# One product for two groups, the third group's scan first, and dt*u in halves

## The chip, the cores and the metric

The kernel runs on one core of one Trainium2 chip. The metric is the device time of one execution in microseconds (us). Engine names are those of the profile: PE is the matmul engine, DVE the vector engine, ACT the scalar engine, POOL is GpSimd, and SP issues nearly all DMAs.

## The reference, cut to what matters

The network has four layers on four images of 56 x 56 pixels and 96 channels. Layers 0 and 1 hold a selective scan; layers 2 and 3 hold linear attention and a quantized feed-forward part. Nearly all the time goes to the scans, and the change is in them. For each image the 3136 tokens are scanned in four directions, with 192 inner channels and 16 states a channel:

```python
d_a = jnp.exp(dt[..., None] * a)                 # decay, one per channel, state, token
d_b = dt[..., None] * b_ssm[:, :, None, :]
def step(h, inp):
    da_t, db_t, x_t, c_t = inp
    h = da_t * h + db_t * x_t[..., None]         # h = decay*h + (dt*u)*B
    y_t = jnp.einsum('bds,bs->bd', h, c_t)       # y = sum over states of h*C
```

The outputs of the four directions are added and go on to the gates, projections and normalizations of the layer.

## The kernel before, in words

**Chunks and rounds.** A direction's 3136 tokens are cut into 7 chunks of 448 tokens. Two layers, four images, four directions and seven chunks make 224 chunks. Each chunk has eight *rounds* r = 0..7: the two halves e of the inner channels (96 each) times the four quarters q of the states. A round handles 32 channels x 4 states on the 128 partitions, for NG = 3 *groups* of channels. So there are 1792 rounds, and two of the four directions read the image by columns (`orient` 1), where `U` is read with a stride.

**One round n, in `scans`.** `products(n)` multiplies du (that is dt*u, spread over the partitions) by B for the groups 0 and 1 on DVE; B lies in the PSUM bank `b`, where PE put it (`spread_b`, line 606). Group 2's product is made on POOL, one round ahead, in `begin(n + 1)` (line 699), with B and C from the tile `cb` in SBUF. `scan(n, g)` (line 711) runs the recurrence on DVE for g = 0, 1, 2, in place in the tile `h`, with the decays from the PSUM bank `da[g]`; after each scan ACT makes the next round's decay of that group in the same bank (`decay`, line 663). After the third scan ACT keeps the last column (`kept`, line 681) and later puts it in front of the next chunk's tile (`carried`, line 676). POOL then multiplies h by C for all three groups at once (line 753, tile `hc`), and two rounds later PE adds the states up (`add_up`, line 784) behind a filling of matmuls on zeros (`keep_busy`, line 771).

**The order is written out by hand.** DVE, PE, ACT and POOL take their instructions in the order of the program, each in one queue. In a round POOL's queue holds: line 753 of the round before, then whatever `prepare` put there, then line 699 for the next round, then line 753 of this round. Line 753 waits for the round's last scan.

**What is prepared ahead.** For every chunk `prepare(ch, o)`, `prepare_on_scalar(ch, o)` and `on_tensor(ch, o)` are called with o from -14 up: o = -1 is the last round before the chunk's first. At o = -7 and -6 ACT makes dt = softplus in the tile `dtc` (two Exp and, at -6, one Ln over both halves, line 498). At o = -5 `times_u` makes `duc` = dt*u on POOL, both halves in one instruction of 96 x 896 elements (line 511), and `park` sends `dtc` to DRAM in three DMAs of SP. At o = -4 `duc` is parked likewise. `spread_dt` and `spread_du` fetch both back onto 128 partitions, for e = 0 at -4 and -3, for e = 1 at 0. `fetch` brings `cb` at -3 to 0. In terms of the chunk in front, o = -6, -5, -4, -3 are its rounds 2, 3, 4, 5.

**Work beside the rounds.** The rest of the network runs as *lanes*: generators that are moved on at the `yield` of each half round, as far as a planner's budget for ACT and PE allows. Their instructions stand between the scans of DVE, and in the queues of the others.

Of the kernel before, what the change touches and what calls it, by code (L numbers as in the profile page):

```python
# [11 lines left out]
F32 = mybir.dt.float32  # L12
# [4 lines left out]
ALU = mybir.AluOpType  # L17
# [3 lines left out]
HS = 56  # L21
L = HS * HS
C = 96
DI = 192
NS = 16
NE = 2
NG = 3
NQ = 4
# [4 lines left out]
CS = 448  # L33
# [134 lines left out]
class Net:  # L168
# [333 lines left out]
        t = self.sp.tile([rows, 2 + n * CS], F32, name=name, bufs=bufs)  # L502
        return t[:, 2:].rearrange("p (n t) -> p n t", t=CS)

    def times_u(self, ch):

        ch.duc = self.sp.tile([C, NE, CS], F32, name="duc", bufs=1)
        u = self.both.rearrange("p e (h w) -> p e w h" if ch.orient else "p e (h w) -> p e h w", w=HS)
        lo = ch.c * CS // HS
        in_rows = lambda t: t.rearrange("p e (a b) -> p e a b", b=HS)  # L510
        self.nc.gpsimd.tensor_tensor(in_rows(ch.duc), in_rows(ch.dtc), u[:, :, lo : lo + CS // HS], ALU.mult)  # L511

    def park(self, t):
        d = self.dram.tile([NE, 32, NG, CS], F32, tag="dd", name="dd", bufs=6)
        for g in range(NG):
            self.nc.sync.dma_start(d[:, :, g].rearrange("e d t -> d e t"), t[32 * g : 32 * g + 32])
        return d

    def spread(self, t, d):
# [25 lines left out]
    def prepare(self, ch, o):  # L545

        nc = self.nc
        if o == -14:  # L550
            self.parameters(ch)
        elif o == -12:
            self.inputs(ch)
        elif o == -9:
            ch.cd = self.dram.tile([2 * NS, CS], F32, tag="cd", name="cd", bufs=3)
            nc.sync.dma_start(ch.cd, ch.cf[: 2 * NS])
        elif o == -5:
            self.times_u(ch)
            ch.dtd = self.park(ch.dtc)
        elif o == -4:  # L560
            ch.dud = self.park(ch.duc)
            self.spread_dt(ch, 0)
        elif o == -3:
            self.spread_du(ch, 0)
        elif o == 0:
            self.spread_du(ch, 1)
            self.spread_dt(ch, 1)
        if -3 <= o <= 0:
            self.fetch(ch, o + 3)
# [43 lines left out]
    def scans(self):  # L613

        nc, sp = self.nc, self.sp
        chunks = []
        for l in range(2):
            for i in range(NB):
                for n, (orient, rev) in enumerate(ORDER[l]):
                    for step in range(NCS):
                        ch = Step()
                        ch.l, ch.i, ch.orient, ch.rev, ch.step = l, i, orient, rev, step
                        ch.k = 2 * orient + rev if l == 0 else orient + 2 * rev
                        ch.c = NCS - 1 - step if rev else step  # L630
                        ch.n, ch.first = n, n == 0 and step == 0
                        ch.skip = n == 0
                        ch.last = n == 3 and step == NCS - 1
                        ch.cb, ch.dt, ch.du = [], [], []
                        chunks.append(ch)
        rounds = [(ch, e, q) for ch in chunks for e in range(NE) for q in range(NQ)]
        per = NE * NQ


        da = [self.psum.tile([128, 512], F32, name=f"da{g}")[:, : CS + 4] for g in range(NG)]  # L640
        for t in da:
            nc.vector.memset(t, 0.0)

        def steps(n):

            return [(ch, n - per * j) for j, ch in enumerate(chunks[max(0, n // per) : n // per + 3], max(0, n // per))]

        def ahead(n):
            for ch, o in steps(n):
                self.on_tensor(ch, o)  # L650

        for n in range(-14, 0):
            for ch, o in steps(n):
                self.prepare(ch, o)
            for ch, o in steps(n):
                self.prepare_on_scalar(ch, o)
            ahead(n)

        def decay(n, g):

            if n < len(rounds):
                ch, e, q = rounds[n]
                nc.scalar.activation(da[g][:, INNER], ch.dt[e][:, g], AF.Exp, scale=ch.par.na[:, e, q, g : g + 1])  # L663

        def column(t, at):

            return t[:, at : at + 2 * ROW + 1 : ROW]

        def carried(n):

            if n < len(rounds):
                ch, e, q = rounds[n]
                hs[n] = sp.tile([128, WIDE], F32, name="h", bufs=3)
                if not ch.step:
                    return
                nc.scalar.copy(column(hs[n], ROW if ch.rev else 1), ch.par.carry[:, e, q])  # L676

        def kept(n):
            ch, e, q = rounds[n]
            if ch.step < NCS - 1:  # L680
                nc.scalar.copy(ch.par.carry[:, e, q], column(hs[n], 2 if ch.rev else CS + 1))  # L681

        def own(n):
            ch, e, q = rounds[n]
            return NQ * e + q in (OWN_TAIL if ch.l and ch.i else OWN)

        hs, bs = {}, {}

        def tokens(t):

            return self.groups(t, 2)[:, :, :CS]

        def begin(n):

            if n < len(rounds):
                ch, e, q = rounds[n]
                bs[n] = self.spread_b(ch, q)
                if not own(n):
                    nc.gpsimd.tensor_tensor(tokens(hs[n])[:, 2], ch.du[e][:, 2], ch.cb[q][:, 1], ALU.mult)  # L699

        def products(n):
            ch, e, q = rounds[n]
            for g in range(3 if own(n) else 2):
                nc.vector.tensor_tensor(tokens(hs[n])[:, g], ch.du[e][:, g], bs[n], ALU.mult)  # L704

        def scan(n, g):
            ch, e, q = rounds[n]
            c = 1 if ch.step else 0
            way = slice(CS + 1 + c, 1, -1) if ch.rev else slice(2 - c, CS + 2)
            h = hs[n][:, g * ROW :]  # L710
            nc.vector.tensor_tensor_scan(h[:, way], da[g][:, way], h[:, way], 0.0, ALU.mult, ALU.add)  # L711

        carried(0)
        carried(1)
        begin(0)
        self.exp_and_ln()
        self.tables = True
        for g in range(NG):
            decay(0, g)
        late = []  # L720
        for n, (ch, e, q) in enumerate(rounds):
            r = NQ * e + q
            products(n)
            for c, o in steps(n):
                self.prepare(c, o)
            self.half_round()
            strided = [1.5 + 1.5 * ch.orient] * (r % NQ == 2)
            strided += [1.5 + 1.5 * c.orient for c, o in steps(n) for _ in self.projected(c, o)]
            self.spend((0.6, 0.7, 1.7, 0, 0, 0, 0.7, 0.6)[r], (1.3, 1.3, 0, 0, 0, 0, 0.4, 0.4)[r] + sum(strided))
            yield "F", n, r  # L730
            for c, o in steps(n):
                self.prepare_on_scalar(c, o)
            ended = late.pop(0) if len(late) == 2 else None
            if ended:
                self.keep_busy(ended[2])
            begin(n + 1)
            if ended:
                self.add_up(*ended)
            ahead(n)
            self.half_round()  # L740
            for g in range(NG):
                if g == 1:
                    yield "C", n, r
                if g == 2 and ended and ended[2] == NQ - 1:
                    self.spend(0.6, 0)
                    self.keep_sums(*ended[:3])
                scan(n, g)
                if g == 2:
                    kept(n)
                decay(n + 1, g)  # L750
            carried(n + 2)
            hc = sp.tile([128, NG, CS], F32, name="hc", bufs=3)
            nc.gpsimd.tensor_tensor(  # L753
                hc, tokens(hs[n]), ch.cb[q][:, 0].unsqueeze(1).to_broadcast([128, NG, CS]), ALU.mult,
            )
            late.append((ch, e, q, hc))
            del hs[n], bs[n]
        for ended in late:
            self.add_up(*ended)
        self.keep_sums(ch, e, q)  # L760
        yield "C", len(rounds), 0
# [647 lines left out]
```

## Time and profile before

| | |
|---|---|
| median of 3 runs | 8133.2 us (8116.01 to 8143.82) |
| the profiled execution | 8146.18 us, of which the span from first to last instruction is 8144.5 us |
| busy, share of the span | DVE 92%, PE 88%, POOL 88%, ACT 75% |
| scan phase (116 to 7934 us) | 7818 us; DVE busy 7445 us, POOL 7138 us |
| granted PE clock | 0.901 |
| SP's DMA issues of `dtc` and `duc` to DRAM | 672 each, 112 KB, 2.0 us to landing |

A group's line on the page names the line of the kernel, the engine, the operation, what is written and read, the shapes and the count; after the first bar stand the busy time in us and the mean of one instruction in ns; after the second the idle time of the engine just before it and what ended it. Consecutive DVE instructions overlap in the record, so the distance from start to start is shorter than the duration of one.

### The profile page before, as it was taken

Reading aid. Unit: us, or ns where it says so; the run is one execution under the profiler, and the core shown is the slowest. Engines: PE = TensorE matmul, PEld = TensorE weight load, DVE = VectorE, ACT = ScalarE, POOL = GpSimd, SP = SyncE. Lnnn points to the kernel's source line nnn. Section 1 sums busy time; section 2 is a strip of 40 time slices with the busy share of each in tenths; the row PEclk is TensorE's granted clock in tenths of the full one; section 3 lists DMA queues with packets and bytes.
Section 4 is the critical chain, followed back from the end, with each engine's and each line's share of the span. In section 5 each row is a group of like instructions: output and inputs, shape, how many; then the busy total and the mean of one; then the engine's idle time right before and its main releaser. Section 6 shows DMA issues by size and latency. Waiting matters only on the chain.

```text
span 8144.5 us, 112387 instructions
## 1 busy us (share of the span) xinstructions
PE 7161.1 (88%) x33234; PEld 2500.2 (31%) x33234; DVE 7523.2 (92%) x9600; ACT 6106.9 (75%) x12765; POOL 7170.7 (88%) x3991
## 2 busy tenths in 40 slices
PE   6889988889888988889889889988899988999887
PEld 3333333222332223322332223333233322433233
DVE  5999999999999999999999998999989999899992
ACT  5878877777778767887777866687767877678776
POOL 4999998999999999999989998899978999888980
PEclk8999989889999989999888998888989899888987
DMA  4555655567556655566555665555655556545552
GB/s 152 177 192 192 198 187 182 177 190 231 186 183 192 208 193 179 179 198 197 193 183 178 195 220 173 164 164 169 193 174 168 170 167 195 175 160 165 172 168 66
DMA packets 568237, 1467.47 MB, mean 180 GB/s; under 512 B 108035, under 2 KB 337157, under 8 KB 566757
## 3 DMA queue, kind: packets, MB, share of 16 engines
q1 hardware_dynamic: 566848, 1458.49, 56.0%
q8 instruction: 261, 4.28, 0.2%
q14 instruction: 356, 2.91, 0.1%
q10 hardware_dynamic: 772, 1.80, 0.1%
HBM read 1186.49 MB, written 273.47 MB: 179 GB/s over the span
## 4 chain that ended last, share of the span: by engine, by line
PE 33%; DVE 30%; ACT 17%; issue 13%; POOL 4%; DMA 2%; SPq 0%; DVEq 0%; POOLq 0%; ACTq 0%
DVE h L711 22%; PE y L784 7%; DVE h L704 7%; PE y L771 5%; ACT da L663 5%; PE y L780 4%; PE b L606 3%; POOL hc L753 2%; PE pp L486 2%; ACT L815 2%; PE ps L932 1%; PE pp L440 1%; PE ps L860 1%; PE ps L845 1%; ACT Y L791 1%
## 5 line engine op out<-in xcount | busy, mean ns | idle before, releaser
L711 DVE TENSOR_TENSOR_SCAN h<-da,h 128x449 f32<-128x449 f32 (+1 forms) x5376 | 5517.9, 1076 | 98.5 <-ACT da L663 81.7
L753 POOL TENSOR_TENSOR hc<-h,cb 128x1344 f32<-128x1344 f32 x1792 | 4884.6, 2726 | 617.1 <-DVE h L711 489.7
L663 ACT ACTIVATE da<-dt,na 128x448 f32<-128x448 f32 x5376 | 3354.0, 632 | 1126.1 <-DVE h L711 1095.6
L704 DVE TENSOR_TENSOR h<-du,b 128x448 f32<-128x448 f32 x3584 | 2026.8, 609 | 150.2 <-PE b L606 87.8
L784 PE MATMUL y<-hc,four 128*32 128x448 f32 x14336 | 1917.6, 610 | 17.8 <-POOL hc L753 17.8
L699 POOL TENSOR_TENSOR h<-du,cb 128x448 f32<-128x448 f32 x1792 | 1755.1, 979 | 71.9 <-ACT h L676 26.4
L771 PE MATMUL y<-w,zeros 128*96 128x448 bf16 x5112 | 1420.5, 396 | 0.0
L606 PE MATMUL b<-cf,sel 128*128 128x448 bf16 x1792 | 676.8, 378 | 698.1 <-DVE h L704 691.3
L771 PEld LDWEIGHTS <-zeros 128*96 128x96 bf16 x5112 | 631.1, 134 | 1174.8 <-issue 1014.7
L440 PE MATMUL pp<-U,wd 96*128 96x448 f32 x896 | 667.2, 833 | 11.4 <-issue 4.4
L784 PEld LDWEIGHTS y<-hc,four 128*32 128x32 f32 x14336 | 294.7, 113 | 1198.2 <-issue 687.3
L780 PE MATMUL y<-Y,ident 96*96 96x448 f32 x672 | 540.5, 894 | 36.9 <-ACT Y L791 18.7
L486 PE MATMUL pp<-cf,wd 12*96 12x448 f32 (+1 forms) x896 | 480.8, 618 | 89.7 <-ACT dtc L496 54.0
L681 ACT COPY carry<-h 128x3 f32<-128x3 f32 x1536 | 302.1, 197 | 262.6 <-DVE h L711 256.7
L511 POOL TENSOR_TENSOR duc<-dtc,U 96x896 f32<-96x896 f32 x224 | 483.0, 2156 | 11.1 <-ACT dtc L498 11.1
L791 ACT COPY Y<-y 96x448 f32<-96x448 f32 x448 | 342.0, 763 | 24.2 <-PE y L784 23.0
L676 ACT COPY h<-carry 128x3 f32<-128x3 f32 x1536 | 280.0, 182 | 52.2 <-POOL hc L753 49.3
L496 ACT ACTIVATE dtc<-pp,wd 96x448 f32<-96x448 f32 x448 | 281.5, 628 | 19.3 <-PE pp L486 15.1
L577 ACT COPY cf<-pp 64x448 f32<-64x448 f32 x448 | 235.6, 526 | 79.8 <-PE pp L599 71.5
L606 PEld LDWEIGHTS <-sel 128*128 128x128 bf16 x1792 | 184.3, 103 | 350.8 <-issue 282.2
L845 PEld LDWEIGHTS ps<-avg,w 96*112 96x112 f32 (+2 forms) x1936 | 250.4, 194 | 93.2 <-issue 55.3
L486 PEld LDWEIGHTS pp<-cf,wd 12*96 12x96 f32 (+1 forms) x896 | 114.3, 166 | 471.1 <-ACT dtc L496 163.9
(384 smaller groups left out, 5698.4 us busy)
## 6 DMA issues: line engine op xcount, KB each, us to landing
cb<-cd SPq DMA_DIRECT2D x896, 448.0 KB, 4.5
dt<-dd SPq DMA_DIRECT2D x448, 672.0 KB, 5.7
du<-dd SPq DMA_DIRECT2D x448, 672.0 KB, 5.5
dd<-dtc SPq DMA_DIRECT2D x672, 112.0 KB, 2.0
dd<-duc SPq DMA_DIRECT2D x672, 112.0 KB, 2.0
win<-m SPq DMA_DIRECT2D x252, 112.0 KB, 4.2
U<-u SPq DMA_DIRECT2D x112, 168.0 KB, 4.8
w<-z SPq DMA_DIRECT2D x84, 224.0 KB, 4.0
```

Source lines behind the costliest of these rows:

```text
L440: self.nc.tensor.matmul(ch.ps.rearrange("p (a b) -> p a b", b=HS), ch.par.wx[:, e], self.in_order(self.U[e], ch.orient, ch.c * CS, CS), st ...
L486: self.nc.tensor.matmul(ch.pd, ch.par.wt[rows, C * e : C * e + C], ch.cf[rows], start=True, stop=True)
L511: self.nc.gpsimd.tensor_tensor(in_rows(ch.duc), in_rows(ch.dtc), u[:, :, lo : lo + CS // HS], ALU.mult)
L606: self.nc.tensor.matmul(ps, self.sel[:, q], self.upper(ch.cf), start=True, stop=True)
L663: nc.scalar.activation(da[g][:, INNER], ch.dt[e][:, g], AF.Exp, scale=ch.par.na[:, e, q, g : g + 1])
L699: nc.gpsimd.tensor_tensor(tokens(hs[n])[:, 2], ch.du[e][:, 2], ch.cb[q][:, 1], ALU.mult)
L704: nc.vector.tensor_tensor(tokens(hs[n])[:, g], ch.du[e][:, g], bs[n], ALU.mult)
L711: nc.vector.tensor_tensor_scan(h[:, way], da[g][:, way], h[:, way], 0.0, ALU.mult, ALU.add)
L753: nc.gpsimd.tensor_tensor(hc, tokens(hs[n]), ch.cb[q][:, 0].unsqueeze(1).to_broadcast([128, NG, CS]), ALU.mult,)
L771: self.nc.tensor.matmul(self.y[:C], self.zeros[:, :C], self.some, start=False, stop=False)
L780: nc.tensor.matmul(o, w, self.in_order(a, ch.orient, ch.c * CS, CS), start=True, stop=False)
L784: nc.tensor.matmul(self.y[32 * n : 32 * n + 32], self.four, hc[:, g], start=n == 3, stop=n == 3 or q == NQ - 1,)
```

## The change

In each round DVE makes the product of the groups 0 and 1 in one instruction of 128 x 2 x 448, with B repeated by a step of zero. The scans run in the order 2, 0, 1 in place of 0, 1, 2; all that hangs on a place in this loop (`kept`, `keep_sums`, the lanes' turn) keeps its place. `times_u` is split into one instruction of 96 x 448 for each half, at o = -6 and -5, and stands in POOL's queue behind line 699 of that round instead of in front of it. `park` is split into halves too, both still in the same step: six DMAs of 56 KB in place of three of 112 KB, for `dtc` and for `duc`.

```diff
-    def times_u(self, ch):
-        ch.duc = self.sp.tile([C, NE, CS], F32, name="duc", bufs=1)
...
-        self.nc.gpsimd.tensor_tensor(in_rows(ch.duc), in_rows(ch.dtc), u[:, :, lo : lo + CS // HS], ALU.mult)
+    def times_u(self, ch, e):
+        if e == 0:
+            ch.duc = self.sp.tile([C, NE, CS], F32, name="duc", bufs=1)
+        in_rows = lambda t: t[:, e].rearrange("p (a b) -> p a b", b=HS)
+        u = self.in_order(self.U[e], ch.orient, ch.c * CS, CS)
+        self.nc.gpsimd.tensor_tensor(in_rows(ch.duc), in_rows(ch.dtc), u, ALU.mult)
 
-    def park(self, t):
-        d = self.dram.tile([NE, 32, NG, CS], F32, tag="dd", name="dd", bufs=6)
+    def park(self, t, e, d=None):
+        if e == 0:
+            d = self.dram.tile([NE, 32, NG, CS], F32, tag="dd", name="dd", bufs=6)
         for g in range(NG):
-            self.nc.sync.dma_start(d[:, :, g].rearrange("e d t -> d e t"), t[32 * g : 32 * g + 32])
+            self.nc.sync.dma_start(d[e, :, g], t[32 * g : 32 * g + 32, e])
...
         elif o == -5:
-            self.times_u(ch)
-            ch.dtd = self.park(ch.dtc)
+            ch.dtd = self.park(ch.dtc, 0)
+            self.park(ch.dtc, 1, ch.dtd)
         elif o == -4:
-            ch.dud = self.park(ch.duc)
+            ch.dud = self.park(ch.duc, 0)
+            self.park(ch.duc, 1, ch.dud)
             self.spread_dt(ch, 0)
...
+        def u_products(n):
+            for ch, o in steps(n):
+                if o in (-6, -5):
+                    self.times_u(ch, o + 6)
...
         def products(n):
             ch, e, q = rounds[n]
-            for g in range(3 if own(n) else 2):
-                nc.vector.tensor_tensor(tokens(hs[n])[:, g], ch.du[e][:, g], bs[n], ALU.mult)
+            m = 3 if own(n) else 2
+            b = bs[n].unsqueeze(1).to_broadcast([128, m, CS])
+            nc.vector.tensor_tensor(tokens(hs[n])[:, :m], ch.du[e][:, :m], b, ALU.mult)
...
             begin(n + 1)
+            u_products(n)
...
-            for g in range(NG):
-                if g == 1:
+            for at, g in enumerate((2, 0, 1)):
+                if at == 1:
                     yield "C", n, r
-                if g == 2 and ended and ended[2] == NQ - 1:
+                if at == 2 and ended and ended[2] == NQ - 1:
                     self.spend(0.6, 0)
                     self.keep_sums(*ended[:3])
                 scan(n, g)
-                if g == 2:
+                if at == 2:
                     kept(n)
                 decay(n + 1, g)
```

More of the change, by code (lines that the diff above doesn't have):

```diff
@@ L503, in shifted @@
         return t[:, 2:].rearrange("p (n t) -> p n t", t=CS)
-    def times_u(self, ch):
-        ch.duc = self.sp.tile([C, NE, CS], F32, name="duc", bufs=1)
[L508 to L511, printed above, removed]
-    def park(self, t):
-        d = self.dram.tile([NE, 32, NG, CS], F32, tag="dd", name="dd", bufs=6)
+    def times_u(self, ch, e):
[7 more added lines that the diff above has]
+            d = self.dram.tile([NE, 32, NG, CS], F32, tag="dd", name="dd", bufs=6)
         for g in range(NG):
-            self.nc.sync.dma_start(d[:, :, g].rearrange("e d t -> d e t"), t[32 * g : 32 * g + 32])
+            self.nc.sync.dma_start(d[e, :, g], t[32 * g : 32 * g + 32, e])
         return d
@@ L736, in scans @@
             begin(n + 1)
+            u_products(n)
             if ended:
```

## The prediction

> **What bounds the kernel now.** I read the page first (busy shares, costliest groups), then DVE's and POOL's rows in order of time on a stretch without lane work, then the waits. The groups:
>
> ```profile
> PE 7161.1 (88%) x33234; PEld 2500.2 (31%) x33234; DVE 7523.2 (92%) x9600; ACT 6106.9 (75%) x12765; POOL 7170.7 (88%) x3991
> L711 DVE TENSOR_TENSOR_SCAN h<-da,h 128x449 f32<-128x449 f32 (+1 forms) x5376 | 5517.9, 1076 | 98.5 <-ACT da L663 81.7
> L753 POOL TENSOR_TENSOR hc<-h,cb 128x1344 f32<-128x1344 f32 x1792 | 4884.6, 2726 | 617.1 <-DVE h L711 489.7
> L704 DVE TENSOR_TENSOR h<-du,b 128x448 f32<-128x448 f32 x3584 | 2026.8, 609 | 150.2 <-PE b L606 87.8
> L699 POOL TENSOR_TENSOR h<-du,cb 128x448 f32<-128x448 f32 x1792 | 1755.1, 979 | 71.9 <-ACT h L676 26.4
> ```
>
> DVE is first, but POOL is close behind: its three jobs a round are nearly as long as DVE's five. The timeline shows how close, over the rounds 2 to 5 of a chunk read by columns; DVE's rows:
>
> ```profile
> 1718.49 1.13 DVE L704 TENSOR_TENSOR h<-du,b 128x448 f32<-128x448 f32 x2
> 1719.53 3.06 DVE L711 TENSOR_TENSOR_SCAN h<-da,h 128x449 f32<-128x449 f32 x3
> 1722.50 1.13 DVE L704 TENSOR_TENSOR h<-du,b 128x448 f32<-128x448 f32 x2
> 1723.54 3.06 DVE L711 TENSOR_TENSOR_SCAN h<-da,h 128x449 f32<-128x449 f32 x3
> 1726.51 1.13 DVE L704 TENSOR_TENSOR h<-du,b 128x448 f32<-128x448 f32 x2
> ```
>
> and POOL's in the same stretch:
>
> ```profile
> 1718.71 2.73 POOL L753 TENSOR_TENSOR hc<-h,cb 128x1344 f32<-128x1344 f32 x1 [0.90 <-DVE h L711]
> 1721.41 0.97 POOL L699 TENSOR_TENSOR h<-du,cb 128x448 f32<-128x448 f32 x1
> 1722.73 2.73 POOL L753 TENSOR_TENSOR hc<-h,cb 128x1344 f32<-128x1344 f32 x1 [0.35 <-DVE h L711]
> 1725.42 2.58 POOL L511 TENSOR_TENSOR duc<-dtc,U 96x896 f32<-96x896 f32 x1
> 1727.96 0.98 POOL L699 TENSOR_TENSOR h<-du,cb 128x448 f32<-128x448 f32 x1
> 1728.89 2.73 POOL L753 TENSOR_TENSOR hc<-h,cb 128x1344 f32<-128x1344 f32 x1
> ```
>
> DVE repeats a gapless round of 4.01 us (1722.50 to 1726.51). POOL waits for the last scan, needs 3.63 us (1718.71 to the end of line 699, less the overlap of rows) and is idle 0.35 us. The waits say the same: DVE stands little.
>
> ```profile
> DVE h L704 <- PE b L606: 87.8, 87, 2.9
> DVE h L711 <- ACT da L663: 81.7, 172, 2.2
> SPq L516 <- POOL duc L511: 930.5, 216, 7.6
> ```
>
> From the starts of the single instructions, the medians in a round are: product to product 512 ns, product to first scan 531, first to second scan 1002, second to third 983, third scan to next product 983; in all 4011. The scan phase holds 1792 rounds of 4362 ns on average, so some 350 ns a round are lane work and waits. In 407 rounds DVE stands over 40 ns for another engine.
>
> **The joint product (gain).** The rows 602 ns for 96x448 (line 874) and 236 ns for 97x97 (line 1310) give (602 - 236)/(448 - 97) = 1.043 ns an element. The product's 512 ns are then 467 + 45 fixed, and a joint one is 2 x 467 + 45 = 979 against 1024: 45 ns saved. The second scan loses its own wait: of the scans before, two wait for a DVE product and each is 19 ns later than its neighbours (531 against 512, 1002 against 983). After, only group 0's scan has such a wait, so 19 ns more: 64, a round of 3947. Bounds: 45 if the joint product, which now waits for PE and ACT in one place, loses the 19 again. Of the repeated operand no row exists on DVE from PSUM; the cast on line 360, with a repeated SBUF operand, took 219 ns for 128 elements against 198 for a plain 96 (line 409), 0.7 ns an element, so I take no penalty; the far end, an element at the scan's 2.1 ns, would lose 0.9 us a round and stands as a rival. A round that waits for PE or ACT anyway keeps nothing: 1385 x 64 ns = **89 us** (at 45 ns 62; if all rounds kept it 115).
>
> The Trainium skill (VectorE: DVE Perf Modes, "The TRN2 errata") gives a whole fp32 tensor_tensor as (N + 151)/0.96 ns: 624 for one product, near the 609 here, and 1091 for the joint one. Taking these as times to the next start, 157 ns a round or 281 us would go. The trace does not agree: the next instruction starts 97 ns before the recorded end of the one in front.
>
> **Scan 2 first (cost).** Line 699 must now be done when the joint product is, 0.98 us into the round, not some 3 us in. In a quiet round line 699 ends 3.89 us after the round's start (median); it is needed at 3.947 + 0.979 = 4.93, less 0.04 for the signal: a margin of 1.00 us. Had duc stayed whole in front (line 699 ending at 1728.94 above, the first scan starting at 1727.55), this scan would stand 1.4 us. Behind the product, a half duc delays only line 753 and what follows.
>
> A half: lines 699 and 753 give 105 ns fixed (979 for 448, 2726 for 1344). duc takes 1.77 us by rows and 2.54 by columns, so a half (x - 105)/2 + 105 = 0.93 and 1.32, to the next start 0.04 less: 0.89 and 1.28. From both sides: the fixed part could vanish (0.1 less), or a half could cost what other 448-element rows do, up to 1.13 (line 1033), 0.2 more. POOL has 3947 - 3615 = 0.33 us spare a round. After the half in round 2 it is late by 1.28 - 0.33 = 0.95 (rows: 0.56), inside the margin. After round 3's half: 1.90 (1.12). Against 1.00 the scan of round 5 stands **0.90 us by columns, 0.12 by rows**; DVE's scans 0 and 1, next products and ACT's decays queue behind it. If all 224 chunks were quiet: 112 x 1.02 = 114 us.
>
> They are not: whatever else stretches DVE's rounds 2 to 4 gives POOL time. Subtracting each chunk's recorded excess over 3 x 4.01 us leaves 48 us. Counting only the excess of rounds 3 and 4, since what comes in round 2 comes mostly before POOL is late, leaves 56. The first half also comes a round earlier than duc did, and waits for the Ln on line 498: in 56 chunks Ln ended after POOL would have been there, by 72 us in sum. Added chunk by chunk, 48 becomes 57 and 56 becomes 81. I take **81 us**. Lane products on POOL (28 pairs, lines 1033 and 1034, 2.18 us to the next start) exceed spare and margin by 0.85 us: 0 to 24, I take **8**.
>
> **Parks in halves.** SP issues 1344 DMAs more. A park took 0.42 us an issue for 64 rows and never under 0.30; twelve of 0.30 to 0.42 against six of 0.42 add 1.1 to 2.5 us of SP a chunk, with the second half of duc some 0.6 us later. The spread behind it is safe: it is issued 10.4 us (median) before round 7 and lands in 5.7. Lane loads queue behind it on SP: the chain of waits passes through some 20 loads of 3 to 7 us, each up to 2 us later: 0 to 40, I take **10**. The Trainium skill (DMA: Bandwidth & Descriptors, "Bandwidth") speaks against this part: it wants DMAs of 1 MiB and calls those under 64 KB overhead, and these fall to 56 KB. The row sets it at 2.0 us to landing for 112 KB, off the path; the bytes and rows are the same.
>
> At no cost: the decays turn with the scans (2, 0, 1 each), so each bank has the same time; `kept` keeps its place behind the third scan; line 753's new wait for line 699 is for an instruction two back on its queue; PE gets bank `b` free at 1.07 us, as before at 1.12. Cover gone, the waits for PE and ACT above (170 us) grow.
>
> **The sum.** -89 + 81 + 8 + 10 = +10 on 8146: 8156. That execution is 13 us above the median of the runs: **8143 us**. No change, up to 0.3% (24 us, about what a measurement of this kernel can tell from none), is the forecast: the saving is paid back by a wait for POOL.
>
> **Rivals.** *The saving stays* (0.30): the new stalls take the place of waits for PE and ACT (249 us of idle time before products and scans), so only 30 to 50 us are added. For it: a quarter of the rounds last over 4.5 us. -89 + 40 = -49: 8084; with 115 kept and 48 stalled 8066.
> *POOL's turn is dearer* (0.27): halves at 1.13 us or more, or a clogged Ln. Two halves 0.2 dearer make round 5's stall 0.52 by rows and 1.30 by columns: 204 us if all is quiet, 107 with Ln less each chunk's excess; with 18 for lanes and loads +36 to +133: 8169 to 8266, taken 8190. It decides from some 103 us of waits for POOL on. Against it: by rows duc is cheaper an element than line 699.
> *SP becomes late* (0.10): the loads at 40 us and cb or du behind them: -89 + 81 + 8 + 40 = +40, so 8173.
> *The repeated operand is slow* (0.02): 1792 x 0.9 us more, some 9700 us.
> The forecast has 0.31.
>
> **Range and chances.** From the saving stayed to the dearer turn: 8058 to 8225. Faster 0.30, same 0.31, slower 0.39.
>
> **What would show it.** A joint product with the next scan 0.98 us behind it, a quiet round of 3.95, and 0.9 us stalls of line 711 <- POOL 699, in round 5 of column chunks above all: 70 to 110 us in the waits. I am wrong if that wait sums to under 40 or over 150, if half a duc exceeds 1.0 and 1.4 us, or if a product's start follows PE or ACT by much more than before.

## The result, and the profile after

The changed kernel takes 8164.9 us (median of 5 runs, 8161.0 to 8170.6) against 8133.2 us: a ratio of 1.004, 95% interval 1.0023 to 1.0058. The saving on DVE came as forecast, and the new wait for POOL took all of it and 0.4% more.

The page of the changed kernel shows fewer instructions on DVE, 100 us less busy time there, and a new name in the scan's idle time:

```profile
PE 7185.3 (88%) x33234; PEld 2514.2 (31%) x33234; DVE 7421.9 (91%) x7808; ACT 6115.4 (75%) x12765; POOL 7204.7 (88%) x4215
L720 DVE TENSOR_TENSOR_SCAN h<-da,h 128x449 f32<-128x449 f32 (+1 forms) x5376 | 5502.8, 1071 | 223.5 <-POOL h L707 106.7
L763 POOL TENSOR_TENSOR hc<-h,cb 128x1344 f32<-128x1344 f32 x1792 | 4885.1, 2726 | 520.9 <-DVE h L720 395.9
L713 DVE TENSOR_TENSOR h<-du,b 128x896 f32<-128x896 f32 x1792 | 1902.0, 1061 | 149.6 <-PE b L608 58.1
L707 POOL TENSOR_TENSOR h<-du,cb 128x448 f32<-128x448 f32 x1792 | 1755.0, 979 | 77.9 <-ACT h L684 27.4
L511 POOL TENSOR_TENSOR duc<-dtc,U 96x448 f32<-96x448 f32 x448 | 525.1, 1172 | 81.2 <-ACT dtc L498 75.9
```

Lines have moved: 704 is now 713 (the joint product), 711 is 720, 699 is 707, 753 is 763. The scan's idle time rose from 98.5 to 223.5 us.

Now the timeline of DVE over the rounds 2 to 5 of a chunk read by columns, in a stretch without other work (start, duration, operation, and in brackets the idle time before):

```profile
3909.48 1.06 DVE L713 TENSOR_TENSOR h<-du,b 128x896 f32<-128x896 f32 x1
3910.45 3.05 DVE L720 TENSOR_TENSOR_SCAN h<-da,h 128x449 f32<-128x449 f32 x3
3913.42 1.06 DVE L713 TENSOR_TENSOR h<-du,b 128x896 f32<-128x896 f32 x1
3914.40 3.05 DVE L720 TENSOR_TENSOR_SCAN h<-da,h 128x449 f32<-128x449 f32 x3
3917.37 1.06 DVE L713 TENSOR_TENSOR h<-du,b 128x896 f32<-128x896 f32 x1
3918.38 3.06 DVE L720 TENSOR_TENSOR_SCAN h<-da,h 128x449 f32<-128x449 f32 x3
3921.36 1.06 DVE L713 TENSOR_TENSOR h<-du,b 128x896 f32<-128x896 f32 x1
3923.31 3.06 DVE L720 TENSOR_TENSOR_SCAN h<-da,h 128x449 f32<-128x449 f32 x3 [0.90 <-POOL h L707]
```

and POOL's in the same stretch:

```profile
3912.42 0.97 POOL L707 TENSOR_TENSOR h<-du,cb 128x448 f32<-128x448 f32 x1
3913.35 1.36 POOL L511 TENSOR_TENSOR duc<-dtc,U 96x448 f32<-96x448 f32 x1
3914.69 2.72 POOL L763 TENSOR_TENSOR hc<-h,cb 128x1344 f32<-128x1344 f32 x1
3917.38 0.97 POOL L707 TENSOR_TENSOR h<-du,cb 128x448 f32<-128x448 f32 x1
3918.32 1.35 POOL L511 TENSOR_TENSOR duc<-dtc,U 96x448 f32<-96x448 f32 x1
3919.64 2.71 POOL L763 TENSOR_TENSOR hc<-h,cb 128x1344 f32<-128x1344 f32 x1
3922.31 0.97 POOL L707 TENSOR_TENSOR h<-du,cb 128x448 f32<-128x448 f32 x1
```

The reader can see the whole case here. A quiet round, one without other work or waits, is 3.95 us (3913.42 to 3917.37; the commonest distance between two joint products is 3948 ns). The scan follows the joint product after 0.98 us. POOL's product for round 4 ends at 3918.35, just when DVE wants it, and the scan starts at 3918.38. The second half delays line 763 once more, the next product ends at 3923.28, and the scan that could have begun at 3922.34 begins at 3923.31. No idle time stands on POOL in this stretch: it has become the engine that sets the pace for two rounds.

The waits of the changed kernel:

```profile
DVE h L720 <- POOL h L707: 106.7, 147, 3.7
DVE h L720 <- ACT da L671: 99.0, 159, 2.3
POOL duc L511 <- ACT dtc L498: 75.9, 52, 5.7
DVE h L713 <- PE b L608: 58.1, 61, 4.6
```

This view counts idle time between two records, from 150 ns up, and consecutive records overlap. Counted instead as the time by which the scan starts later than its usual distance behind the instruction in front, from 40 ns up, the scan's wait for POOL's product is 127 us in the changed kernel and 16 in the kernel before. Round 5 holds 84 of the 127 (2 before), the other rounds 43 (14 before). These fuller sums are used below, where nothing else is said.

**Where the time went.** Between the two profiled executions the span grows by 18.4 us (8144.5 to 8162.9): 14.7 in the scan phase, 3.7 ahead of it and behind it. In the scan phase DVE's own distances shrink by 1792 x 64 ns = 115 us, the wait for POOL grows by 111, and what is left, 19 us, goes to DVE's other waits. The likely reason, not shown round by round, is that a round with another wait can't keep the saving.

### The profile page after: what moved, and what is told of

Its sections match the earlier page's. It is cut to its first block, busy times and chain, and to the rows that moved or that the text cites. A ratio compares the mean times of both kernels' runs of the same rounds, so it can differ in the third digit from the quotient of the medians.

```text
span 8162.9 us, 113062 instructions
## 1 busy us (share of the span) xinstructions
PE 7185.3 (88%) x33234; PEld 2514.2 (31%) x33234; DVE 7421.9 (91%) x7808; ACT 6115.4 (75%) x12765; POOL 7204.7 (88%) x4215
## 4 chain that ended last, share of the span: by engine, by line
PE 44%; DVE 22%; ACT 13%; issue 11%; POOL 6%; DMA 3%; SPq 0%; DVEq 0%; POOLq 0%; ACTq 0%
DVE h L720 15%; PE y L794 9%; PE y L781 8%; DVE h L713 7%; PE y L790 5%; ACT da L671 4%; PE b L608 4%; POOL hc L763 3%; PE pp L486 2%; PE pp L440 2%; PE ps L870 2%; PE ps L855 2%; PE ps L942 2%; PE ps L819 2%; POOL h L707 1%
## 5 line engine op out<-in xcount | busy, mean ns | idle before, releaser
L720 DVE TENSOR_TENSOR_SCAN h<-da,h 128x449 f32<-128x449 f32 (+1 forms) x5376 | 5502.8, 1071 | 223.5 <-POOL h L707 106.7
L713 DVE TENSOR_TENSOR h<-du,b 128x896 f32<-128x896 f32 x1792 | 1902.0, 1061 | 149.6 <-PE b L608 58.1
L511 POOL TENSOR_TENSOR duc<-dtc,U 96x448 f32<-96x448 f32 x448 | 525.1, 1172 | 81.2 <-ACT dtc L498 75.9
L870 PEld LDWEIGHTS ps<-ident,rs 112*96 112x96 f32 x1744 | 222.0, 191 | 130.0 <-issue 93.6
```

What stands on the lines that cost most here:

```text
L713: nc.vector.tensor_tensor(tokens(hs[n])[:, :m], ch.du[e][:, :m], b, ALU.mult)
```

## Experiments

All times stand against the kernel before on the same chip (8138 to 8140 us there). The forecast gave two theories a place: a saving of 64 ns a round against waits for POOL, or something else behind the time (SP's issues, Ln, no saving at all).

### The joint product alone

```diff
-            for g in range(3 if own(n) else 2):
-                nc.vector.tensor_tensor(tokens(hs[n])[:, g], ch.du[e][:, g], bs[n], ALU.mult)
+            m = 3 if own(n) else 2
+            b = bs[n].unsqueeze(1).to_broadcast([128, m, CS])
+            nc.vector.tensor_tensor(tokens(hs[n])[:, :m], ch.du[e][:, :m], b, ALU.mult)
```

> The kernel before with the joint product alone: scans in the order 0, 1, 2, dt*u whole and in front of line 699, parks whole. Group 0's scan now reads what the instruction just in front of it writes. Theory (the order 2, 0, 1 is there to cover this): the scan starts only after the joint product's end at 1061 ns and a signal, some 1100 to 1150 ns behind its start instead of 979; with 983 for each scan a quiet round is 4.05 to 4.10 us against 4.01, so 8190 to 8260 us, slower, and no wait for line 699. Rival (no cover needed, the joint product is the whole gain): the scan follows at 998 ns, a quiet round of 3.95 us and 8030 to 8060 us, since POOL's product is then wanted late, as before.

8291.9 us, ratio 1.019 (1.0167 to 1.0213). DVE's timeline in a quiet stretch:

```profile
3962.69 1.06 DVE L705 TENSOR_TENSOR h<-du,b 128x896 f32<-128x896 f32 x1
3963.85 3.06 DVE L712 TENSOR_TENSOR_SCAN h<-da,h 128x449 f32<-128x449 f32 x3
3966.83 1.06 DVE L705 TENSOR_TENSOR h<-du,b 128x896 f32<-128x896 f32 x1
```

The scan that reads the joint product starts 1165 ns behind its start (median), 103 ns after the recorded end, where an independent scan starts after 979: 186 ns lie open. The quiet round is 4.14 us. The theory is right in kind and too low in size (it had up to 1150 ns and 8260 us); the rival falls. So the order 2, 0, 1 is no ornament: in the order 0, 1, 2 the joint product costs 1.9%.

### The order 2, 0, 1 alone

```diff
-            for g in range(NG):
-                if g == 1:
+            for at, g in enumerate((2, 0, 1)):
+                if at == 1:
...
```

> The kernel before with the scans in the order 2, 0, 1 alone: two products, dt*u whole and in front of line 699, parks whole. Theory (POOL's product is wanted some 2 us earlier and dt*u stands in front of it): in a quiet chunk the scan of round 4 stands 1.4 us where dt*u reads columns and 0.6 us where it reads rows, 224 us if all chunks were quiet, some half to two thirds of that in fact: 110 to 160 us of waits of the scan for line 699, all in round 4; 8230 to 8290 us. Rival (POOL's place does not matter, the time of the changed kernel comes from SP's additional DMAs): within 20 us of the kernel before.

8305.1 us, ratio 1.0202 (1.0184 to 1.0219), a little beyond the theory's range. The waits:

```profile
DVE h L711 <- POOL h L699: 176.1, 188, 2.1
```

So POOL's place does matter: with dt*u whole and in front of its product, the earlier deadline costs some 170 us. By the fuller sum the waits are 197 us, 159 of them in round 4. With dt*u in halves behind POOL's product the next run is 91 us faster.

### The changed kernel with two products

```diff
-            m = 3 if own(n) else 2
-            b = bs[n].unsqueeze(1).to_broadcast([128, m, CS])
-            nc.vector.tensor_tensor(tokens(hs[n])[:, :m], ch.du[e][:, :m], b, ALU.mult)
+            for g in range(3 if own(n) else 2):
+                nc.vector.tensor_tensor(tokens(hs[n])[:, g], ch.du[e][:, g], bs[n], ALU.mult)
```

> The changed kernel with the two products of before in place of the joint one. Theory (a saving of 64 ns a round against waits for POOL): a quiet round of 3.99 us (512 + 512 + 1002 + 983 + 983), 19 ns less than before; POOL has 0.04 us more to spare a round, so its waits fall from 127 to about 100 us; in all 8180 to 8215 us, slower than both kernels. Rival (the joint product brought nothing on the path): within 10 us of the changed kernel's 8165.

8214.2 us, ratio 1.0089 (1.0072 to 1.0107): 49 us above the changed kernel, at the upper edge of what was expected. The scan's waits for POOL fall to 101 us, as expected. The joint product is on the path. One detail was wrong: the quiet round is 4.01 us, not 3.99. The first scan still follows the second product after 531 ns, though it reads no product of DVE. So the 19 ns are not the price of a wait for a DVE product, as the forecast had it: they go with the pair of short products, and all 64 ns come with the joint one.

### Whole parks

```diff
-            ch.dtd = self.park(ch.dtc, 0)
-            self.park(ch.dtc, 1, ch.dtd)
+            ch.dtd = self.park(ch.dtc)
...
-            ch.dud = self.park(ch.duc, 0)
-            self.park(ch.duc, 1, ch.dud)
+            ch.dud = self.park(ch.duc)
```

> The changed kernel with the parks whole again: three DMAs of 112 KB in place of six of 56 KB, 1344 issues fewer on SP; all else as changed. Theory (waits for POOL and nothing else pay the saving back): within 10 us of the changed kernel's 8165, and the same waits of the scan for line 699 (127 us). Rival (SP's additional issues delay the lanes' loads, the 10 us of the forecast up to its 40): 8125 to 8155 us.

8158.9 us, ratio 1.0028 (1.0017 to 1.0039): 6 us below the changed kernel, with intervals that overlap, and the same 127 us of waits for POOL. SP's issues are not where the time went.

### Both halves a round later

The next three move the halves. Only the two values of o and the step of the second half's park differ.

```diff
-                if o in (-6, -5):
+                if o in (-5, -4):
```

> The changed kernel with both halves one round later, at o = -5 and -4 and still in neighbouring rounds; the second half is parked at -3. This takes away the wait of the first half for Ln (76 us on POOL) and leaves the two halves together. Theory: Ln is behind a fifth to a third of the scan's 127 us of waits, the nearness of the halves behind the rest, now in round 6: 85 to 105 us of waits, 8125 to 8150 us. Rival (Ln is what matters): waits under 45 us, 8060 to 8090.

8171.7 us, ratio 1.0039 (1.0027 to 1.0051); the scan waits 171 us for POOL, 121 of it in round 6. POOL's wait for Ln is gone, and the time is no better. But a new wait has come on POOL (a line of the waits, and one of these waits in the timeline):

```profile
POOL duc L511 <- DMA U<-u: 40.3, 6, 10.5
1979.27 1.35 POOL L511 TENSOR_TENSOR duc<-dtc,U 96x448 f32<-96x448 f32 x1 [10.52 <-DMA U<-u]
```

All images use one tile `U`. `inputs` has SP load the next image's u into it twelve rounds before that image's first round, which is o = -4 of the last chunk of the image in front. In the changed kernel both halves of that chunk stand ahead of these loads. At o = -4 the second half stands behind them in the program, so it waits for them, and it reads the next image's u. That happens in seven chunks; the scans behind them stand 3.5 to 11.0 us each, 54 us in all (the view puts one of POOL's seven waits down to another load). Without these stands the scan waits 117 us for POOL against 127 in the changed kernel, 67 of it in round 6 against 84 in round 5. So the run doesn't show the later place to be worse, the theory misses by 12 us of waits and not by 66, and the rival (under 45 us) falls. The kernel before has a little less other work there: beyond 4.01 us a round, the rounds 2 to 4 of its chunks together last 1242 ns longer in the mean, the rounds 3 to 5 only 978.

The runs below with the second half at o = -3 or -2 also read the next image's u in these seven chunks. Their times tell what the places of the halves do to the waits; none of them is a finished kernel.

### Halves apart, late

```diff
-                if o in (-6, -5):
+                if o in (-5, -2):
...
+        elif o == -1:
+            self.park(ch.duc, 1, ch.dud)
```

> The changed kernel with the two halves of dt*u moved on and apart: the first at o = -5 (round 3), the second at o = -2 (round 6), each behind line 699; the first half is parked at -4 as before, the second at -1, in front of the fetch that needs it at 0. Theory (the second half comes before POOL has caught up, and the first waits for Ln): POOL is late by 0.97 us by columns after the first half, has 0.33 us to spare in each of three rounds, and is on time for the second; the waits of the scan for line 699 fall from 127 us to under 35, the saving of the joint product stays, 8050 to 8090 us. Rival (POOL is short of time on the whole, at 88% busy and more in the scan phase, wherever the halves stand): waits stay over 80 us and the time over 8130.

8107.5 us, ratio 0.9959 (0.9945 to 0.9974); 85 us of waits. The theory holds in direction, not in its numbers: 32 us of the waits lie in round 0, behind the second half, and 24 in round 5. The sum counted one round too many: between rounds 3 and 6 lie two, so POOL, late by 1.00 us after the first half, is still late by 0.33 when the second comes, and then by 1.33 against a margin of 0.98. That gives 0.35 us, and by columns the four stalls of round 0 in chunks without other work are 0.34 to 0.36 us. Six more are 0.97 to 1.00 us; in them POOL has a product of other work between the two halves. Four stalls at the loads of U make 9 of the 32 us. For round 5 the sum gives next to nothing (1.00 against 0.98), and 21 of the 24 us there come within two rounds of other work's products on POOL.

### Halves apart, early

```diff
-                if o in (-6, -5):
+                if o in (-6, -2):
...
+        elif o == -1:
+            self.park(ch.duc, 1, ch.dud)
```

> The changed kernel with the first half where it is (o = -6, waiting for Ln) and the second at o = -2, parked at -1. This leaves the wait for Ln and takes the halves apart. Theory: waits of the scan for line 699 of 30 to 55 us, 8070 to 8105 us. Rival (Ln is what matters): waits of 90 us or more, 8130 to 8165.

8065.3 us, ratio 0.9908 (0.9890 to 0.9927): 0.9% faster than the kernel before, the best of all runs that have dt*u. The waits:

```profile
DVE h L721 <- ACT da L672: 112.5, 171, 3.0
POOL duc L511 <- ACT dtc L498: 71.9, 50, 5.7
DVE h L721 <- POOL h L708: 54.2, 53, 2.2
```

By the fuller sum the scan waits 62 us for POOL, 65 less than in the changed kernel, while POOL still waits 72 us for Ln. The theory had 30 to 55 us and 8070 to 8105; the rival, that Ln matters, falls. The time fell by 100: other waits of DVE shrink too.

A part of the gain may hang on the loads of U. Here SP issues them first and the second half follows; in the changed kernel, whose rows are the last two, it is the other way round:

```profile
1956.53 7.55 SPq L469 DMA_DIRECT2D U<-u  x14
1968.57 1.36 POOL L511 TENSOR_TENSOR duc<-dtc,U 96x448 f32<-96x448 f32 x1 [0.82 <-PE pp L602]
1970.39 1.37 POOL L511 TENSOR_TENSOR duc<-dtc,U 96x448 f32<-96x448 f32 x1
1973.69 8.09 SPq L469 DMA_DIRECT2D U<-u  x14
```

The seven chunks in which these loads are issued take 13 us less than in the changed kernel (227.5 against 240.4 us), of 98 us in the whole scan phase. A kernel that loads U only after the second half may not keep these 13 us; none was run.

### No dt*u at all

```diff
-            ch.dud = self.park(ch.duc, 0)
-            self.park(ch.duc, 1, ch.dud)
+            ch.dud = self.park(ch.dtc, 0)
+            self.park(ch.dtc, 1, ch.dud)
...
-                if o in (-6, -5):
-                    self.times_u(ch, o + 6)
+                pass
```

> The changed kernel without the product dt*u: dt is parked and spread in its place, by as many DMAs. POOL is freed of 525 us. It bounds what any place of the halves can bring. Theory: waits of the scan for line 699 under 20 us, all from lane products; a time of 8040 to 8070 us, 64 ns a round below the kernel before less what rounds with other waits keep. Rival (waits for PE and ACT take over as the rounds get shorter): over 8100.

8050.4 us, ratio 0.9888 (0.9870 to 0.9906), with 30 us of waits for POOL (the theory had under 20). dt is parked and spread in the place of dt*u, so the kernel leaves the product with u out. It bounds what any place of the halves can reach: -6 and -2 are 15 us above it. It also reads no U on POOL, and the seven chunks with the loads of U take 226.2 us here. Of the 30 us of waits that remain without any half, 27 come within two rounds of other work's products in POOL's queue.

### Three rounds apart, early

```diff
-                if o in (-6, -5):
+                if o in (-6, -3):
...
+        elif o == -2:
+            self.park(ch.duc, 1, ch.dud)
```

> The changed kernel with the first half of dt*u at o = -6 and the second at o = -3 (round 5), parked at -2. Apart by three rounds, as in the run with -5 and -2 (85 us of waits of the scan for line 699, 8107 us), with the first half where the run with -6 and -2 has it (62 us, 8065 us). Theory (rounds 2 to 4 hold more of the other work that gives POOL time than rounds 3 to 6, so the place of the first half decides): 55 to 75 us of waits, 8060 to 8085 us. Rival (it is the distance of three rounds in place of four): 80 to 95 us of waits, 8095 to 8115 us.

8089.4 us, ratio 0.9939 (0.9927 to 0.9952), 83 us of waits, 43 of them in round 7. The waits are in the rival's range, the time lies between the two ranges. But four stalls at the loads of U make 14 of the 43 us; without them 70 us of waits are left, which is in the theory's range. So the run doesn't decide between the place and the distance. Where chunks read columns the median of the stalls in round 7 is 0.36 us. Here the sum with two rounds in between fits: 1.33 against 0.98.

### Ln for each half

```diff
-        if e == NE - 1:
-            scalar.activation(ch.dtc, ch.dtc, AF.Ln, bias=1.0)
+        scalar.activation(ch.dtc[:, e], ch.dtc[:, e], AF.Ln, bias=1.0)
```

> The kernel with the halves at o = -6 and -2, with Ln made for each half behind its Exp, at o = -7 and -6, in place of one Ln over both at -6. The first half of dt*u then waits for work that ACT does a round earlier; ACT gets 224 instructions more, some 0.15 us each. If Ln's lateness matters: POOL's wait for it falls from 72 to under 15 us, the scan's waits for line 699 from 62 to 40 to 50 us, and the time by 10 to 20 us to 8045 to 8055. If not (POOL, when it waits there, is early): the wait on POOL falls all the same and the time stays within 8 us of 8065.

8101.6 us, ratio 0.9952 (0.9940 to 0.9965), on top of the halves at -6 and -2. POOL's wait for Ln falls from 72 to 13 us, as both theories had it, but the scan's waits for POOL fall by 4 us only, from 62 to 58. The time goes up instead: ACT has 54 us more to do (6112 to 6167 us busy), and the scan waits longer for it:

```profile
DVE h L720 <- ACT da L671: 132.4, 187, 2.4
DVE h L720 <- POOL h L707: 51.7, 49, 2.4
```

With the halves apart, Ln's lateness was not on the path. Why 54 us of ACT cost 36 us of time was not pursued.

### dt parked whole

```diff
-            ch.dtd = self.park(ch.dtc, 0)
-            self.park(ch.dtc, 1, ch.dtd)
+            ch.dtd = self.park_whole(ch.dtc)
```

> The kernel with the halves at o = -6 and -2, with dt parked whole: three DMAs of 112 KB in place of six of 56 KB, 672 issues fewer on SP. If SP's issues cost nothing on the path: within 6 us of that kernel's 8065. If each costs its 0.3 us in the lanes' loads that queue behind: 10 to 20 us less.

8078.5 us, ratio 0.9927 (0.9913 to 0.9940), against 0.9908 (0.9890 to 0.9927) for the same kernel with half parks. The intervals overlap: the 10 to 20 us are excluded, no difference is not.

### The far halves alone

```diff
-            for at, g in enumerate((2, 0, 1)):
+            for g in range(NG):
...
-            nc.vector.tensor_tensor(tokens(hs[n])[:, :m], ch.du[e][:, :m], b, ALU.mult)
+                nc.vector.tensor_tensor(tokens(hs[n])[:, g], ch.du[e][:, g], bs[n], ALU.mult)
```

> The kernel before with the halves of dt*u at o = -6 and -2 behind line 699, parked in halves, but two products and the scans in the order 0, 1, 2. It tells what the earlier relief of POOL is worth without the joint product and the earlier scan. Theory: line 699 was never late before (16 us of waits), so nothing is gained: 8125 to 8150 us. Rival (a part of the 73 us between the kernel before and the one with the halves at -6 and -2 comes from POOL's smoother queue): 8095 to 8120 us.

8123.0 us, ratio 0.9975 (0.9965 to 0.9986). Between the two ranges: the halves at -6 and -2 bring some 16 us by themselves, though the scan hardly waited for POOL before. Between the profiled executions the gain is 20 us, and 11 of it lie in the seven chunks in which the loads of U are issued (228.3 against 239.0 us), so more than half may hang on these loads no longer waiting for the second half. What brings the rest was not settled. The other 58 us of the 0.9% come with the joint product and the order.

## Why the prediction came out as it did, step by step

**The joint product** was sized right. From start to start 979 ns were forecast and measured, and the quiet round is 3948 ns against 3947. Of its two parts the 19 ns were explained wrongly (the run with two products) without harm to the sum. The forecast let 89 of the 115 us stay, since 407 rounds wait anyway; by the trace it is 115 - 19 = 96, if the other waits' 19 us are counted against it.

**The margin** of 1.00 us and the stalls in quiet chunks were right in the main (POOL has two jobs in every round and dt*u once in eight rounds, not three jobs a round): 0.90 was forecast by columns in round 5, and of the 13 chunks that are quiet there the middle half has 0.94 to 1.00; by rows 0.12, and the median of 30 quiet chunks is 0.24.

**The wait for POOL is the mis-sized term**: 81 + 8 us forecast, 111 measured, counted as above and less the kernel before. Round 5, where the two halves make the scan stand, took 82 of it, against 81 forecast. The other rounds took 28, against 8 forecast for the lanes' products. So the term that was too small is the one for stalls outside round 5: of the 43 us that they come to in all, 30 lie within two rounds of other work's products on POOL. The run without dt*u points the same way, with 30 us of waits without any half, where the kernel before has 16.

That round 5 came out at 82 is in part luck, since two prices in it were too low. A half costs 0.98 and 1.37 us (forecast 0.93 and 1.32): two of them take 187 to 189 ns more than the whole (1767 and 2543 ns), where 105 were taken from other rows. And line 763 starts 170 ns after the last scan's end, not 145, which takes 25 ns of the margin. By these the quiet stalls are 2 x (1.33 - 0.33) - 0.98 = 1.02 and 0.24 us, together 24% more than the forecast's 1.02 a pair, which would have made 100 us of the 81. Something else was reckoned too high by as much. The 24 us that the sum gave to Ln (57 to 81) are one candidate: in the changed kernel the chunks in which POOL waits for Ln hold only 16 of round 5's 84 us. Too small a credit for other work is the other; the runs don't part the two.

**Parks** stood at 10 us, 0 to 40; the whole parks put them at 6, within what the runs can tell from none.

**The sum** was 8156 for the profiled execution, which took 8164.6: 8 us off. The step from there to the medians took away 13 us, as the profiled execution of before lay that far above its median; the changed kernel's does not, and so the forecast of 8143 is 22 us low. About half of the 13 us was chance: the kernel before, run again beside the experiments, has medians of 8138 to 8140. The mechanism forecast, the saving paid back by a wait for POOL, is what happened; the end lies 0.1% beyond its bound of 0.3%, towards the dearer turn of POOL, the rival with that sign. The rival in which the saving stays falls for this kernel; with the halves at -6 and -2 the time falls to 8065, where it had forecast 8084 (8066 at best), though up to 13 us of that may hang on the loads of U.

**Rules of the skill.** The Trainium skill (VectorE: DVE Perf Modes, "The TRN2 errata") gives, as an estimate by its formula, (896 + 151)/0.96 = 1091 ns for the joint product; its record is 1061. As a distance between starts it holds for neither case: 979 when the next scan is independent, 1165 when it reads the product. The same page ("The DRAIN you can't avoid") reports that a semaphore after each of eight chained copies cost nothing extra; here a scan that waits for the product just in front of it starts 186 ns later than one that doesn't, so the measurement decides.

## What to carry to other kernels

When an instruction is made wider, ask what reads it next: here a consumer directly behind it waited for its end and 0.1 us more, so an independent instruction belonged in between, and that one's own producer then had a new deadline. Work that an in-order queue does once in eight rounds should be spread by what the queue has to spare a round, not put in neighbouring rounds: here 0.33 us a round against halves of 0.9 to 1.3 us, and moving the second half three rounds further took the scan's waits from 127 to 62 us and turned 0.4% slower into 0.9% faster. A half of the data that is needed later can be made later, but only as long as its inputs are still there: here the tile `U` was loaded anew in between, and up to 13 us of the gain may hang on that.

## What was not expected of the hardware

A DVE scan that reads the instruction just in front starts 103 ns after that instruction's recorded end (1165 against 1062), where an independent one starts 82 ns before it (979 against 1061). A scan behind a 448-element product starts 19 ns later than another product would (531 against 512), also where it reads no product of DVE; behind the 896-element product the 979 ns are those of the estimate without these 19. An issue of SP took the same 0.42 us for 56 KB as for 112 KB (medians 419 and 420 to 427 ns), and the landing 1.7 us against 2.0.
